# Newton-Schulz sets of a two-layer kernel: turned tiles only streamed, and each turn one transfer to memory and one back

## The chip, the cores and the metric

The kernel runs on one core of a Trainium2 chip. The metric is the device time of one execution in microseconds (us); of the kernel before there are three runs, and one more execution that was profiled.

## The reference

Two layers act on `x` of shape (32, 32, 128, 128) in float32: 32 batches of 32 channels, each channel a 128x128 matrix. The first layer is the one that the change touches. Per matrix it computes an approximate matrix square root by five Newton-Schulz steps:

```python
A2 = gn(x).reshape(b * c, 128, 128)        # group norm over pairs of channels
normA = sqrt(sum(A2 * A2)); Y = A2 / normA; Z = I
for _ in range(5):
    T = 0.5 * (3.0 * I - Z @ Y)
    Y = Y @ T
    Z = T @ Z
x = x + Y * sqrt(normA)
```

The second layer is a spectral convolution: a group norm, a 2-D Fourier transform of which 32 x 64 frequencies are kept, a product over channels with two weight tensors, the inverse transform and a sum with `x`.

## The kernel before, in words

**Sets.** The first layer goes by sets of four channels: a tile is [128 rows, 4, 128]. There are 32 x 8 = 256 sets. The five steps are folded into a few products per set (`newton`, line 447): a quartic polynomial `q` of the matrix, `y = q m`, the next matrix `m = q y`, a second quartic, a last product pair and `t`. A product needs one factor with its rows as the contracted dimension, so at some points a matrix is needed in transposed form. `products` (line 345) runs four 128x128 matmuls into one of eight accumulator banks (`bank`, line 179); its first argument is stationary in TensorE, its second is streamed. In the profile's names `ps<-my,q` the streamed tile stands first and the stationary one second. Each float32 matmul stands in the profile as two instructions, so one call of `products` is 8 of them.

**Near and far.** Batches 1 to 18 are *far* (`is_far`, line 357): 144 sets. The other 112 are *near* and transpose on TensorE. A far set has the transposition done by VectorE and the DMA queues. VectorE transposes within 32x32 blocks straight from the accumulator bank into a tile `turn` (`across`, line 420), and four DMAs of 64 KB on SyncE's queue then move each group of 32 partitions of `turn` to its place in `w` or `mb`. There are three such trips in a far set: one in each of its two quartics (`far_quartic`, line 431, into `w`) and one for the next matrix (line 464, into `mb`). `w` keeps its blocks side by side and is read by TensorE as a strided stream; `mb` is laid out straight, since it is used as a stationary factor, so its transfers write runs of 32 floats.

**Subtractions.** GpSimd computes `eye - matrix` (`minus`, line 340): once in `staged` (line 402), twice in place on the second factor, once on the next matrix (line 466). VectorE adds a product to it (line 436) and forms `q`, `t` and the sum with `x` (`plus`, line 329).

**Order.** Every instruction stays in the order in which the program issues it, per engine. The main loop (line 1090) makes rounds over 8 lanes; a lane holds one set and takes one step of its generator per round, to the next `yield`. `rest` is two yields. A far set has 23 yields and a new one starts every `FAR` = 23/8 rounds. So the yields between two instructions of a set say how many rounds of other work lie between them. From a transposition to the product that streams or holds its result there are four in every trip. `settle` (line 496) stores the finished set to `mid` on SyncE's queue, and loads of `x` go on ScalarE's queue (`fetch`, line 366). Buffers of a tile's name rotate by the numbers in `rooms` (line 308), the second number being extra ones for the first part of the kernel.

**The end of a set.** One 256-wide streamed matmul (line 478) multiplies `q` with `y` and `m` together into two banks, ScalarE takes `m`'s half in two pieces (`t`) and `y`'s in four, and two more products end the set.

Of the kernel before, what the change touches and what calls it, by code (L numbers as in the profile page):

```python
# [29 lines left out]
F32 = mybir.dt.float32  # L30
AF = mybir.ActivationFunctionType
ALU = mybir.AluOpType
# [4 lines left out]
P = 128  # L37
# [11 lines left out]
MS = 1 / QR  # L49
# [44 lines left out]
def conv_preact_kernel(  # L94
# [19 lines left out]
    nc.vector.tensor_scalar_mul(eye1[:, 0, :], ident, EYE)  # L114
    eye = eye1.to_broadcast([P, 4, P])
    eyes = []
    for n, f in (("v", EYE_V), ("q", EYE_Q), ("p", EYE_Q * TURNED)):
        e = const.tile([P, 1, P], F32, name=f"eye_{n}")
        nc.vector.tensor_scalar_mul(e[:, 0, :], ident, f)
        eyes.append(e.to_broadcast([P, 4, P]))  # L120
# [98 lines left out]
    def kept(issued):  # L219
        return issued  # L220

    def prep(bs, made):

        n = len(bs)
        nc_, ng = n * C, n * G
        first_b = bs[0]
        st = small.tile([P, ng, 6], F32, tag="a_st", name=f"a_st{first_b}", bufs=2)
        tiles = []
        parts = [(b, i) for b in bs for i in range(C // 4)]

        ahead = 3 if first_b else 8

        def load(k):
            b, i = parts[k]
            if first_b or i < 4:
                t = stp.tile([P, 2, 2 * P], F32, tag="xs", name=f"xs{b}_{i}")
            else:
                t = four("turn", True).rearrange("p (j c) x -> p j (c x)", j=2)
            src = xs_in[b, :, 2 * i : 2 * i + 2].rearrange("p g h c -> p g (h c)")
            kept(nc.scalar.dma_start(out=t, in_=src))  # L240
            tiles.append(t)

        for k in range(ahead):
            load(k)
        yield
        for k in range(len(parts)):
            for j in range(2):
                nc.vector.bn_stats(st[:, 2 * k + j, :], tiles[k][:, j, :])
            yield
            if k + ahead < len(parts):  # L250
                load(k + ahead)
        ms = small.tile([P, ng], F32, tag="a_ms", name=f"a_ms{first_b}")
        nm, d = yield from moments(st, ms, "a")
        yield from pause
        pq = bank()[:, 0, 0:nc_]
        nc.tensor.matmul(pq, avg_mean, d.rearrange("p g c -> p (g c)"), start=True, stop=True)
        if not first_b:
            warm(5)

        v = small.tile([P, nc_ + ng], F32, tag="a_v", name=f"a_v{first_b}")  # L260
        nc.vector.tensor_scalar_mul(v[:, 0:nc_], pq, -512 / (P * P))
        yield
        vg = small.tile([P, ng], F32, tag="a_vg", name=f"a_vg{first_b}")
        nc.vector.tensor_reduce(
            vg, v[:, 0:nc_].rearrange("p (g c) -> p g c", c=2), AX.X, ALU.add
        )
        nc.vector.tensor_scalar(v[:, nc_:], vg, 0.5, EPS, ALU.mult, ALU.add)
        yield
        s = small.tile([P, nc_ + ng], F32, tag="a_r_s", name=f"a_r_s{first_b}", bufs=2)
        yield from root(v, nc_ + ng, s)  # L270
        iv = small.tile([P, nc_ + ng], F32, tag="a_inv", name=f"a_inv{first_b}")
        nc.vector.reciprocal(iv, s)
        yield

        sc = small.tile([P, nc_], F32, tag="a_sc", name=f"a_sc{first_b}", bufs=2)
        nc.vector.tensor_scalar_mul(sc, iv[:, 0:nc_], MS / P)
        off = small.tile([P, ng, 2], F32, tag="a_off", name=f"a_off{first_b}", bufs=2)
        nc.vector.tensor_tensor(
            off,
            sc.rearrange("p (g c) -> p g c", c=2),  # L280
            nm[:, :, None].to_broadcast([P, ng, 2]),
            ALU.mult,
        )
        off = off.rearrange("p g c -> p (g c)")
        sn = small.tile([P, nc_], F32, tag="a_t_s", name=f"a_t_s{first_b}", bufs=3)
        for k, b in enumerate(bs):
            g, c = slice(k * G, k * G + G), slice(k * C, k * C + C)
            made[b] = (nm[:, g], sc[:, c], off[:, c], sn[:, c])
        yield
        nn = small.tile([P, ng, 2], F32, tag="a_d", name=f"a_n{first_b}")  # L290
        nc.vector.tensor_tensor(
            nn,
            s[:, 0:nc_].rearrange("p (g c) -> p g c", c=2),
            iv[:, nc_:, None].to_broadcast([P, ng, 2]),
            ALU.mult,
        )
        nn = nn.rearrange("p g c -> p (g c)")
        for far in sorted({is_far(b) for b in bs}):
            of = [k for k, b in enumerate(bs) if is_far(b) == far]
            c = slice(of[0] * C, of[-1] * C + C)  # L300
            f = EYE_Q * QS * TURNED**2 if far else EYE * QF
            nc.vector.tensor_scalar_mul(nn[:, c], nn[:, c], P * (1.5 / f) ** 2)
        yield
        yield from root(nn, nc_, sn)
        yield


    rooms = dict(b=(4, 4), xt=(10, 4), x=(3, 2), r=(4, 0), v=(3, 4), w=(3, 2), q=(4, 2))
    rooms.update(my=(4, 2), mb=(2, 3), t=(3, 2), y4=(2, 2), turn=(0, 4))
    turns = dict.fromkeys(rooms, 0)  # L310

    def four(tag, more):
# [27 lines left out]
    def minus(eye, m, t):  # L340

        nc.gpsimd.tensor_tensor(t, eye, m, ALU.subtract)
        return t
# [13 lines left out]
    def is_far(b):  # L357
        return 0 < b < FIRST
# [15 lines left out]
    def staged(b, g, nm, sc, off, sn):  # L374
# [10 lines left out]
        for j in range(4):  # L385
# [13 lines left out]
                on_scalar(m[:, j, :], xt[:, j, :], off, sc, c)  # L399
            on_scalar(mb[:, j, :], mb[:, j, :], off, sc, c)  # L400
            yield
        v = minus(eye_v, m, four("v", True)) if is_far(b) else None
        ready.append((xt, m, mb, v))
        yield

# [11 lines left out]
        yield from rest  # L417
        return q

    def across(ps, more, into):  # L420


        t = four("turn", more)
        nc.vector.transpose(blocks(t), ps.rearrange("p c (i b) -> p b c i", b=4))
        for a in range(4):
            src = t[32 * a : 32 * a + 32].rearrange("p c x -> p (c x)")
            kept(
                nc.sync.dma_start(out=into(a), in_=src.rearrange("p (b x) -> p b x", b=4))
            )

    def far_quartic(m, mb, v, more, f, eye_q):

        ps = products(mb, m)
        w = four("w", more)
        across(ps, more, lambda a: w.rearrange("p c x -> p (c x)")[:, P * a : P * a + P])
        nc.vector.scalar_tensor_tensor(v, ps, 1 / (9 * MS * f), v, ALU.mult, ALU.add)
        minus(eye_q, mb, mb)
        yield from rest
        yield from rest
        ps = products(v, blocks(w).rearrange("p a c j -> p c a j"))  # L440
        q = plus(ps, 9 / (39 * MS**2), mb, "q", more)
        yield from rest
        return q

# [2 lines left out]
    def newton(g, sn, xt, m, mb, v, far, more):  # L447


        qf = QS if far else QF  # L450
        if far:
            q = yield from far_quartic(m, mb, v, more, 1.0, eye_q)
        else:
            q = yield from near_quartic(m, mb, more)
        my = four("my", more)
        y = my[:, :, 0, :]
        nc.scalar.mul(y, products(q, m), 1 / (MS * qf))
        yield from rest
        m = my[:, :, 1, :]
        ps = products(q, y)  # L460
        nc.scalar.mul(m, ps, MS / qf)
        if far:
            mb = four("mb", more)
            across(ps, more, lambda a: mb[:, :, 32 * a : 32 * a + 32])
            yield from rest
            v = minus(eye_v, m, four("v", more))
            yield from rest
            qf, et, eye_t = QS * TURNED, EYE_Q * TURNED, eye_p
            q = yield from far_quartic(m, mb, v, more, TURNED, eye_p)
        else:  # L470
            yield from rest
            mb = taken(transposed(m), "mb", more)
            yield from rest
            et, eye_t = EYE, eye
            q = yield from near_quartic(m, mb, more)
        both = [bank().rearrange("p (j k) x -> p j k x", k=2) for _ in range(2)]
        for j in range(4):
            nc.tensor.matmul(both[j // 2][:, j % 2], q[:, j], my[:, j], start=True, stop=True)
        w, y = four("t", more), four("y4", more)
        for h in range(2):  # L480
            nc.scalar.mul(w[:, 2 * h : 2 * h + 2, :], both[h][:, :, 1, :], 1 / (MS * qf))
        for j in range(4):
            c = 4 * g + j
            nc.scalar.mul(y[:, j, :], both[j // 2][:, j % 2, 0, :], sn[:, c : c + 1])
        yield from rest
        t = plus(products(w, q), -0.5 * et / (1.5 * qf), eye_t, "t", more)
        yield from rest
        nc.vector.tensor_tensor(xt, products(t, y), xt, ALU.add)
        if not todo and lanes.count(None) == LANES - 1:
            warm(2)  # L490
        yield
# [707 lines left out]
```

## Time and profile before

| | |
|---|---|
| three runs | median 3038.55 us, 3033.91 to 3040.33 |
| the profiled execution's own time | 3030.63 us |
| its span, first to last instruction | 3028.5 us |
| TensorE clock granted, mean | 0.984 |
| busy, PE / weight loads / VectorE / ScalarE / GpSimd | 2856.4 / 2636.7 / 2271.7 / 1567.5 / 1995.5 us |
| DMA packets | 746612, 598.69 MB, mean 198 GB/s |
| far sets, first staged to last transfer | about 80 to 1570 us |

The names on the page are those of the program. All compute instructions carry one line (L88, the helper that keeps the order), so rows are told apart by their tiles. PE is the matmul stream, PEld the weight loads that overlap it. SPq stands for instructions that SyncE's sequencer issues, DMAs above all. The time in a row after the second bar is idle time of that engine just before these instructions, and the arrow names what ended it.

### The profile page before, as it was taken

The page shows a single profiled execution, that of the slowest core. Times are in us where ns is not written, and L with a number is a line of the kernel's source. Part 1 is how long each engine was busy: PE and PEld are TensorE (multiplying, and loading weights), DVE is VectorE, ACT ScalarE, POOL GpSimd, SP SyncE. Part 2 cuts the span into 40 slices and gives each one's busy share as a digit, 9 for nine tenths or more (in the row PEclk, how much of TensorE's full clock was granted, in tenths as well). Part 3 has the DMA queues.
Part 4 walks back from the last instruction along what each step waited for, and adds up shares of the span by engine and source line. Part 5 has one row for each costly group of instructions (what it writes and reads, how often), then busy time and mean ns, then how long its engine had stood idle before and what let it go on. Part 6 is the DMA issues. An engine that isn't in the chain of part 4 may idle for free.

```text
span 3028.5 us, 73234 instructions
## 1 busy us (share of the span) xinstructions
PE 2856.4 (94%) x26536; PEld 2636.7 (87%) x26536; DVE 2271.7 (75%) x4407; ACT 1567.5 (52%) x4043; POOL 1995.5 (66%) x2308
## 2 busy tenths in 40 slices
PE   7999999999999999999999999999989999999996
PEld 7999988989989898898899889888878899888884
DVE  7878787878878787878776645877886867777564
ACT  4555555555545555555544445555554544555452
POOL 4677766777767676777665534787777754678352
PEclk9999999999999999999999999999999999999997
DMA  5577777778676877777753566877867747666676
GB/s 178 153 202 173 197 181 178 185 181 205 165 199 166 210 167 204 171 204 174 199 137 99 160 208 206 269 245 252 274 231 253 246 123 214 214 220 216 179 223 247
DMA packets 746612, 598.69 MB, mean 198 GB/s; under 512 B 403472, under 2 KB 564240, under 8 KB 746256
## 3 DMA queue, kind: packets, MB, share of 16 engines
q1 hardware_dynamic: 632640, 385.56, 46.9%
q10 hardware_dynamic: 113616, 208.45, 21.7%
q8 instruction: 215, 3.52, 0.5%
q14 instruction: 141, 1.16, 0.1%
HBM read 326.93 MB, written 153.62 MB: 159 GB/s over the span
## 4 chain that ended last, share of the span: by engine, by line
PE 51%; DMA 17%; DVE 10%; POOL 9%; issue 5%; SPq 5%; ACT 2%; ACTq 1%; DVEq 0%; POOLq 0%
PE ps L88 51%; SPq L88 5%; DMA w<-turn 4%; DMA mb<-turn 3%; POOL yt L88 3%; DMA yt<-mid 2%; DMA mid<-xt 2%; POOL r L88 2%; POOL fold L88 2%; DVE turn L88 2%; POOL x L88 2%; DMA xs<-in_xs 1%; DVE v L88 1%; DVE yt L88 1%; DVE q L88 1%
## 5 line engine op out<-in xcount | busy, mean ns | idle before, releaser
L88 PE MATMUL ps<-my,q 128*128 128x128 f32 (+1 forms) x4096 | 749.7, 331 | 41.3 <-ACT my L88 21.0
L88 PEld LDWEIGHTS ps<-my,q 128*128 128x128 f32 x4096 | 623.6, 192 | 94.7 <-ACT my L88 23.6
L88 ACT ACTIVATE b<-b,a_off,a_sc 128x128 f32<-128x128 f32 x1024 | 467.9, 491 | 348.3 <-DMA b<-in_x 63.8
L88 PE MATMUL ps<-w,v 128*128 128x128 f32 x4096 | 550.4, 279 | 40.5 <-DVE w L88 15.9
L88 PEld LDWEIGHTS ps<-w,v 128*128 128x128 f32 x4096 | 499.7, 193 | 56.6 <-issue 23.4
L88 POOL TENSOR_TENSOR fold<-xt 128x256 f32<-128x256 f32 x512 | 363.7, 733 | 247.1 <-DVE xt L88 220.6
L88 ACT ACTIVATE my<-ps 128x512 f32<-128x512 f32 x512 | 305.7, 599 | 413.9 <-PE ps L88 386.3
L88 POOL TENSOR_TENSOR yt<-yt,d 128x512 f32<-128x512 f32 x244 | 306.8, 1282 | 221.5 <-ACT d L88 190.5
L88 DVE STREAM_TRANSPOSE turn<-ps 128x512 f32<-128x512 f32 x432 | 302.8, 705 | 178.4 <-ACT my L88 102.1
L88 POOL TENSOR_TENSOR v<-eye_v,x 128x512 f32<-128x512 f32 x144 | 183.6, 1275 | 262.7 <-ACT x L88 255.7
L88 POOL TENSOR_SCALAR x<-xt,a_nm,a_sc 128x128 f32<-128x128 f32 x736 | 324.9, 457 | 15.1 <-DVE a_sc L88 14.8
L88 ACT ACTIVATE t<-ps 128x256 f32<-128x256 f32 x512 | 186.9, 380 | 268.9 <-PE ps L88 255.6
L88 ACT ACTIVATE y<-ps,a_t_s 128x128 f32<-128x128 f32 x1024 | 291.4, 375 | 0.0
L88 PE MATMUL ps<-my,mb 128*128 128x128 f32 x2048 | 275.5, 278 | 10.7 <-DMA mb<-turn 4.8
L88 PE MATMUL ps<-x,b 128*128 128x128 f32 x2048 | 281.3, 280 | 1.1 <-ACT b L88 1.0
L88 PE MATMUL ps<-x,q 128*128 128x128 f32 x2048 | 277.5, 279 | 4.6 <-DVE q L88 2.6
L88 PE MATMUL ps<-q,t 128*128 128x128 f32 x2048 | 275.0, 278 | 6.8 <-ACT t L88 6.2
L88 PEld LDWEIGHTS ps<-my,mb 128*128 128x128 f32 x2048 | 259.8, 193 | 22.1 <-issue 9.1
L88 PE MATMUL ps<-y,t 128*128 128x128 f32 x2048 | 275.0, 278 | 0.3 <-DVE b_r L88 0.3
L88 POOL TENSOR_TENSOR mb<-eye_p,mb 128x512 f32<-128x512 f32 x144 | 184.0, 1278 | 133.1 <-PE ps L88 130.9
L88 PEld LDWEIGHTS ps<-x,q 128*128 128x128 f32 x2048 | 252.2, 194 | 15.9 <-issue 8.4
L88 PEld LDWEIGHTS ps<-q,t 128*128 128x128 f32 x2048 | 251.1, 193 | 9.2 <-ACT t L88 7.3
(132 smaller groups left out, 4776.4 us busy)
## 6 DMA issues: line engine op xcount, KB each, us to landing
w<-turn SPq DMA_DIRECT2D x1152, 64.0 KB
b<-in_x ACTq DMA_DIRECT2D x256, 256.0 KB
xt<-in_xt ACTq DMA_DIRECT2D x256, 256.0 KB
mid<-xt SPq DMA_DIRECT2D x256, 256.0 KB
yt<-mid SPq DMA_DIRECT2D x128, 512.0 KB
xs<-in_xs ACTq DMA_DIRECT2D x252, 256.0 KB
out<-yt SPq DMA_DIRECT2D x115, 512.0 KB
mb<-turn SPq DMA_DIRECT2D x576, 64.0 KB
```

The source lines that it names most:

```text
L88: return self.tc.keep_in_program_order(issue(*args, **kw))
```

## The change

It touches far sets only.

- The roles of the two factors are exchanged in the products of a far set: what was held stationary after a turn is now streamed (`products(mb, m)` becomes `products(m, mb)`), and the subtraction in place is made on the other factor. Tiles that came by a trip (`w`, `mb`) are both kept with their blocks side by side and read through `by_rows`.
- `across` is replaced by three functions: `turned` (the same transposition), `away` (one 256 KB DMA from `turn` to a buffer in memory) and `back` (one 256 KB DMA from there, issued two yields later). Both are on SyncE's queue. 12 buffers in memory rotate.
- In the second quartic the subtraction that makes `v` reads the turned tile by rows, and it is issued with the product in place of two yields ahead of it; the addition on VectorE comes one yield later.
- The 256-wide matmul of far sets becomes two 128-wide products with `q` stationary; ScalarE takes the first in one piece.
- Two more early buffers (`b`, `mb`).

```diff
-    rooms = dict(b=(4, 4), xt=(10, 4), x=(3, 2), r=(4, 0), v=(3, 4), w=(3, 2), q=(4, 2))
-    rooms.update(my=(4, 2), mb=(2, 3), t=(3, 2), y4=(2, 2), turn=(0, 4))
+    rooms = dict(b=(4, 5), xt=(10, 4), x=(3, 2), r=(4, 0), v=(3, 4), w=(3, 2), q=(4, 2))
+    rooms.update(my=(4, 2), mb=(2, 4), t=(3, 2), y4=(2, 2), turn=(0, 4))
...
-        v = minus(eye_v, m, four("v", True)) if is_far(b) else None
+        v = minus(eye_v, mb, four("v", True)) if is_far(b) else None
...
-    def across(ps, more, into):
+    def turned(ps, more):
         t = four("turn", more)
         nc.vector.transpose(blocks(t), ps.rearrange("p c (i b) -> p b c i", b=4))
-        for a in range(4):
-            src = t[32 * a : 32 * a + 32].rearrange("p c x -> p (c x)")
-            kept(
-                nc.sync.dma_start(out=into(a), in_=src.rearrange("p (b x) -> p b x", b=4))
-            )
+        return t
+
+    def away(t):
+        held = dram.tile([P, 512], F32, name="turn", tag="turn", bufs=12)
+        kept(nc.sync.dma_start(out=held, in_=t.rearrange("p c x -> p (c x)")))
+        return held
+
+    def back(held, tag, more):
+        t = four(tag, more)
+        src = held.rearrange("(a i) (b x) -> (i b) a x", a=4, b=4)
+        into = t.rearrange("p c x -> p (c x)").rearrange("p (a x) -> p a x", a=4)
+        kept(nc.sync.dma_start(out=into, in_=src))
+        return t
+
+    def by_rows(t):
+        return blocks(t).rearrange("p a c j -> p c a j")
 
-    def far_quartic(m, mb, v, more, f, eye_q):
-        ps = products(mb, m)
-        w = four("w", more)
-        across(ps, more, lambda a: w.rearrange("p c x -> p (c x)")[:, P * a : P * a + P])
-        nc.vector.scalar_tensor_tensor(v, ps, 1 / (9 * MS * f), v, ALU.mult, ALU.add)
-        minus(eye_q, mb, mb)
-        yield from rest
+    def far_quartic(m, mb, v, f, later, more):
+        ps = products(m, mb)
+        held = away(turned(ps, more))
+        minus(eye_q, m, m)
+        if later:
+            yield
+        nc.vector.scalar_tensor_tensor(v, ps, 1 / (9 * MS), v, ALU.mult, ALU.add)
+        if not later:
+            yield
+        yield
+        w = back(held, "w", more)
         yield from rest
-        ps = products(v, blocks(w).rearrange("p a c j -> p c a j"))
-        q = plus(ps, 9 / (39 * MS**2), mb, "q", more)
+        q = plus(products(v, by_rows(w)), 9 / (39 * MS**2 * f**2), m, "q", more)
         yield from rest
         return q
...
         if far:
-            mb = four("mb", more)
-            across(ps, more, lambda a: mb[:, :, 32 * a : 32 * a + 32])
+            held = away(turned(ps, more))
+            nc.scalar.mul(m, ps, MS / qf)
             yield from rest
-            v = minus(eye_v, m, four("v", more))
+            mb = back(held, "mb", more)
             yield from rest
-            qf, et, eye_t = QS * TURNED, EYE_Q * TURNED, eye_p
-            q = yield from far_quartic(m, mb, v, more, TURNED, eye_p)
+            v = four("v", more)
+            form = "p c (a j) -> p c a j"
+            minus(eye_p.rearrange(form, a=4), by_rows(mb), v.rearrange(form, a=4))
+            q = yield from far_quartic(m, by_rows(mb), v, TURNED, True, more)
+            w, y4 = four("t", more), four("y4", more)
+            nc.scalar.mul(w, products(q, by_rows(mb)), 1 / (MS * qf * TURNED))
+            ps = products(q, y)
+            for j in range(4):
+                c = 4 * g + j
+                nc.scalar.mul(y4[:, j, :], ps[:, j, :], sn[:, c : c + 1])
```

More of the change, by code (lines that the diff above doesn't have):

```diff
@@ L116, in conv_preact_kernel @@
     eyes = []
-    for n, f in (("v", EYE_V), ("q", EYE_Q), ("p", EYE_Q * TURNED)):
+    for n, f in (("v", EYE_V), ("q", EYE_Q), ("p", EYE_V * TURNED)):
         e = const.tile([P, 1, P], F32, name=f"eye_{n}")
@@ L300, in prep @@
             c = slice(of[0] * C, of[-1] * C + C)
-            f = EYE_Q * QS * TURNED**2 if far else EYE * QF
+            f = EYE_Q * QS if far else EYE * QF
             nc.vector.tensor_scalar_mul(nn[:, c], nn[:, c], P * (1.5 / f) ** 2)
@@ L447, in newton @@
     def newton(g, sn, xt, m, mb, v, far, more):
-        qf = QS if far else QF
+        qf, et, eye_t = (QS, EYE_Q, eye_q) if far else (QF, EYE, eye)
         if far:
-            q = yield from far_quartic(m, mb, v, more, 1.0, eye_q)
+            q = yield from far_quartic(m, mb, v, 1.0, False, more)
         else:
@@ L456, in newton @@
         y = my[:, :, 0, :]
-        nc.scalar.mul(y, products(q, m), 1 / (MS * qf))
+        nc.scalar.mul(y, products(q, mb if far else m), 1 / (MS * qf))
         yield from rest
         m = my[:, :, 1, :]
-        ps = products(q, y)
-        nc.scalar.mul(m, ps, MS / qf)
+        ps = products(y, q) if far else products(q, y)
         if far:
-            mb = four("mb", more)
-            across(ps, more, lambda a: mb[:, :, 32 * a : 32 * a + 32])
+            held = away(turned(ps, more))
+            nc.scalar.mul(m, ps, MS / qf)
             yield from rest
-            v = minus(eye_v, m, four("v", more))
+            mb = back(held, "mb", more)
             yield from rest
-            qf, et, eye_t = QS * TURNED, EYE_Q * TURNED, eye_p
-            q = yield from far_quartic(m, mb, v, more, TURNED, eye_p)
+            v = four("v", more)
[8 more added lines that the diff above has]
+                nc.scalar.mul(y4[:, j, :], ps[:, j, :], sn[:, c : c + 1])
         else:
+            nc.scalar.mul(m, ps, MS / qf)
             yield from rest
@@ L473, in newton @@
             yield from rest
-            et, eye_t = EYE, eye
             q = yield from near_quartic(m, mb, more)
[L476 to L484, printed above, removed]
+            both = [bank().rearrange("p (j k) x -> p j k x", k=2) for _ in range(2)]
+            for j in range(4):
+                nc.tensor.matmul(both[j // 2][:, j % 2], q[:, j], my[:, j], start=True, stop=True)
+            w, y4 = four("t", more), four("y4", more)
+            for h in range(2):
+                nc.scalar.mul(w[:, 2 * h : 2 * h + 2, :], both[h][:, :, 1, :], 1 / (MS * qf))
+            for j in range(4):
+                c = 4 * g + j
+                nc.scalar.mul(y4[:, j, :], both[j // 2][:, j % 2, 0, :], sn[:, c : c + 1])
         yield from rest
@@ L487, in newton @@
         yield from rest
-        nc.vector.tensor_tensor(xt, products(t, y), xt, ALU.add)
+        ps = products(y4, t) if far else products(t, y4)
+        nc.vector.tensor_tensor(xt, ps, xt, ALU.add)
         if not todo and lanes.count(None) == LANES - 1:
```

## The prediction

> **What bounds the kernel now.** I read the busy time of the whole span first, then that of a stretch which holds far sets alone (200 to 1500 us), then what TensorE waited for in that stretch, then its rows by shape, and last SyncE's queue.
>
> ```profile
> PE 2856.4 (94%) x26536; PEld 2636.7 (87%) x26536; DVE 2271.7 (75%) x4407; ACT 1567.5 (52%) x4043; POOL 1995.5 (66%) x2308
> ```
>
> ```profile
> 200.00:1500.00 1300.00, 1245.36 (x10202) 1171.38 (x10200) 1065.65 (x2109) 706.66 (x1882) 931.42 (x1027) 0.99 0.75 187
> ```
>
> In the far stretch PE is busy 1245 of 1300 us, VectorE 82%, ScalarE 54%, GpSimd 72%, the 16 DMA engines 75%. The stretch issues 512 of the 576 `mb` transfers, four to a set: 128 sets, 10.16 us each, so a round (one set per 23/8 rounds) is 3.53 us. TensorE sets the pace, and what a change here can give is bounded by the 55 us in which it is idle. Its waits in this stretch:
>
> ```profile
> PE ps L88 <- ACT my L88: 13.6, 7, 3.3
> PE ps L88 <- DMA mb<-turn: 11.8, 9, 3.5
> PE ps L88 <- DVE q L88: 10.0, 11, 1.3
> PE ps L88 <- DMA xt<-in_xt: 5.6, 4, 1.7
> PE ps L88 <- ACT t L88: 3.4, 3, 2.3
> PE ps L88 <- DMA w<-turn: 3.3, 4, 1.8
> ...
> PE ps L88 <- DVE turn L88: 1.8, 1, 1.8
> ```
>
> Columns are us, times, longest. The trips of turned tiles (`mb`, `w`, `turn`) make 16.9 us; with the issue gap at each I count 19. The rows by shape of the same stretch:
>
> ```profile
> L88 PE MATMUL ps<-my,q 128*128 128x256 f32 x1028 | 244.6, 381 | 9.0 <-DVE q L88 8.9
> ...
> L88 PE MATMUL ps<-my,q 128*128 128x128 f32 x1032 | 138.5, 277 | 14.1 <-ACT my L88 13.6 <-DVE v L88 0.4
> L88 PE MATMUL ps<-my,mb 128*128 128x128 f32 x1024 | 137.7, 278 | 10.1 <-DMA mb<-turn 4.8 <-issue 2.0 <-DVE turn L88 1.8
> ```
>
> Mean durations overlap, so I took start-to-start times from the same records: median 112 ns for a 128-wide instruction, 216 ns for a 256-wide one. SyncE's queue in one stretch of the timeline (start, us, what, how many):
>
> ```profile
> 1039.67 3.37 SPq L88 DMA_DIRECT2D mb<-turn  x4
> 1043.14 5.15 SPq L88 DMA_DIRECT2D w<-turn  x8
> 1049.54 3.51 SPq L88 DMA_DIRECT2D mb<-turn  x4
> 1053.10 0.62 SPq L88 DMA_DIRECT2D mid<-xt  x1
> 1054.71 5.10 SPq L88 DMA_DIRECT2D w<-turn  x8
> ```
>
> It issues nearly without a pause: 13 issues of about 0.64 us in a set's 10.16. I matched every transposition with its four issues, their landing (last semaphore step of the DMA) and the product that needs them. Medians for `w`: 2.8 us from the end of the transposition to the first issue, 2.5 for four issues, 1.9 from the last issue to landing, and then 3.2 us of slack until the product (mean 3.1; in 5% of the trips 0.1, which are the waits above). For `mb`: 0.6, 2.8, 2.8 and 3.9 of slack. From transposition to product it is 11.4 us (`w`) and 10.2 (`mb`).
>
> **What the Trainium skill says.** "DMA: Bandwidth & Descriptors", section "Specifications", wants 512 B or more per descriptor for line rate. The trace agrees: in the stretch, packets of 128 B took 13 ns (median), of 512 B 27, of 2 KB 84, which is 10, 19 and 24 GB/s per engine; but a 128 B packet is still the cheapest one to have. The same page, "Latency and other measured facts", gives HBM access as 0.2 us, 2 us at high load. The store `mid<-xt`, 256 KB to memory, landed in 2.3 us at the 5th percentile, 3.4 median, 5.0 at the 95th: a spread of that size. The same page, "Two DMAs through the same engine are not ordered", says that the issuer must wait for the first transfer's semaphore before it issues one that reads what it wrote; so SyncE must wait for each `away`. The trace has no such pair in the turns. "TensorE: Matmul & The Clock Gate", section "Wait — 56ns, not 53.3ns?", puts a fixed 2.5 ns on a matmul; here 2 x 112 - 216 = 8 ns, and I use the 8.
>
> **The change part by part.**
>
> *The split matmul.* Per far set 8 instructions of 216 ns become 16 of 112: +64 ns, on the engine that sets the pace; x 144 = +9 us. Weight loads grow by 8 per set and stay under the stream (PEld 1171 against 1245). Streaming `mb` by rows should be free: `w` was streamed so and has the same 112 ns.
>
> *ScalarE.* Two `t` pieces of 380 ns become one 512-wide of about 599: -0.16 us per set on an engine at 54%: nothing. In staging, `v` now waits for the last `b` piece and not the last `x` piece, 0.5 us; rounds of other work cover it.
>
> *GpSimd.* Four subtractions of 1.28 us before and after. The second `v` is now made with the product rather than two rounds ahead, and VectorE needs it one round (3.5 us) later. GpSimd waited 103.6 us for PE at this place (80 times), so it has room for 1.28 us: nothing, at most 0.5 us for one set in five (14 us). By-rows reading there was not in the trace; equal cost is likely, as inner runs are contiguous.
>
> *VectorE.* Same work: three transpositions (0.71 us), two additions (0.65). The second one a round later holds its bank longer. From a `my,mb` product to the eighth bank request after it is 7.55 us (minimum 6.7). The addition now ends about 0.9 + 3.5 + 0.65 = 5.1 us plus VectorE's lag after the product; that lag is 0.04 us median, 2.0 at the 75th percentile, 3.4 at the 95th. So it is late in about one set in five, by some 0.5 us: 14 us if all count. I take +5, ends 0 and 15. Queued behind a late addition would be the next transposition.
>
> *SyncE's queue.* 12 issues per set become 6: from 13 x 0.64 = 8.3 to 7 x 0.64 = 4.5 us in 10.16. It waits longer instead: `back` waits for its `away` to land, and queued behind it are the next `away`, other sets' `back` and `mid<-xt`.
>
> *DMA engines.* Per set the turns took 1024 packets x 33.8 ns (mean) + 2048 x 13.8 = 63 engine-us (66 by totals per set). Now 3 x (128 x 89.2 + 512 x 33.8) = 86: the share goes from 0.75 to about 0.87 (0.80 if packets took their medians). The byte count of the turns doubles.
>
> *The trip itself*, which decides. Its four rounds are unchanged. In the new order of SyncE's queue, an `mb` return stands behind two later `away`, a `w` return mostly behind one (180 of 240; none in 30, two in 30). SyncE issues in order, so a return cannot go before VectorE has transposed those other sets, however soon its own tile has landed. I laid this order over the instants of the trace before (ends of transpositions, 0.6 us per issue, 3.4 us for a landing in memory as `mid<-xt`, 3.8 for the return as the loads `xt<-in_xt`, median 3.9, and `b<-in_x`, 3.4). The return is then issued 5.7 us (`w`) and 4.8 (`mb`) after the transposition, median, 8.6 and 7.3 at the 95th percentile, and lands 3.8 later. Slack to the product: median 1.6 us for `w`, 2.2 for `mb`, and 95 of 384 trips late, by 60 + 45 = 105 us in all. Before it was 3.2 and 3.9. So the second landing costs more than the six spared issues. The 105 us are not all lost: 3 x 11 / 10.2 = 3.2 trips are in flight at a time, and a stall for one gives the same time to the others. I count a third, 35 us, and take off 10, half of the 19 that trips cost already, since SyncE's backlog behind them goes: +25 in this stretch, x 144/128 = +28. Ends: -21 (all 19 x 1.125 gone) and, if lateness is hardly shared, +110.
>
> *Sum* against the profiled execution: 3030.6 (2.1 above its span, start and end, unchanged) + 9 + 5 + 28 = 3073. The median of the runs stands 8 above that execution: **3081 us**, 1.4% slower.
>
> **The rivals.**
>
> *SyncE's relief wins.* If both legs land near their floor (2.3 and 3.0 us) and VectorE's lag shrinks, returns come in time. Then the 19 us of trip waits go, and half of the waits for `my` and `q` (23.6) that follow from late trips: 31 x 1.125 = 35, less the 9 of the split: 3013, faster. For it: SyncE was busy 8.3 of 10.2 us and 2.8 us behind for `w`, and the same overlay of the old order gives 5 us of slack where the trace had 3.1 to 3.5, so backlog costs more than my overlay tells. Against: the order of the queue holds returns back by a whole transposition of another set. It decides from the point where transposition to landing is under some 8 us (5th percentile of the time until the product: 8.2 for `w`, 7.7 for `mb`).
>
> *The DMA engines become the bound.* At 0.87 share, legs land in 4.0 and 4.5: 125 + 69 = 194 us late, a third is 65, less 10, x 1.125 = 62; the loads come late as well (ScalarE waited 55.5 us for `b<-in_x` already), +20. With 9 and 5: 3135.
>
> *It is hidden anyway.* Trips late as often as now: 9 us of split, less some: 3042, no change.
>
> **How the numbers follow.** Late returns 0.47 (3050 to 3112), DMA-bound 0.15, relief 0.27, hidden 0.11. A measurement of this kernel can tell about 0.2%, 6 us, from no change. Faster 0.27, same 0.11, slower 0.62. Range 3012 to 3150: below lies half of the relief case, above the worst of the DMA-bound one.
>
> **What would show it.** Right: PE waits for `mb<-turn` and `w<-turn` in the far stretch grow from 15 us to 35 or more; SyncE's longest waits are for transpositions, with a return queued behind; the stretch of far sets grows by 35 to 45 us and the rest not at all; DMA share there 0.80 to 0.87; no 256-wide `my,q` rows of far sets; PE waits for `v` appear, a few us. Wrong: slack after landing of 3 us or more; PE waits for DMAs under 10 us; or GpSimd's by-rows subtraction over 1.5 us, which would make VectorE's addition the wait.

## The result and the profile after

| | before | after |
|---|---|---|
| median of the runs | 3036.41 us (4) | 3177.74 us (4; 3157.59 to 3178.41) |
| ratio, 95% interval | | 1.0448, 1.0405 to 1.0491 |
| profiled execution, span | 3028.5 us | 3176.6 us |
| last `mb` transfer of a far set starts | 1558 us | 1698 us |
| a far set, in 200 to 1500 us | 10.16 us (128 sets) | 11.11 us (117 sets) |
| PE idle per far set there | 0.43 us | 1.14 us |
| PE busy per far set there | 9.73 us | 9.97 us |

The change makes the kernel 4.5% slower. The direction was forecast, the size was not: 3177.74 lies above the range. Of the 148 us between the two spans 140 are there by the last `mb` transfer, so the loss is in the far sets. The lines of the profile after that answer to those shown of before, first the busy times of the span, then of the far stretch:

```profile
PE 2900.2 (91%) x27688; PEld 2705.4 (85%) x27688; DVE 2266.5 (71%) x4407; ACT 1558.3 (49%) x3899; POOL 1997.8 (63%) x2308
```

```profile
200.00:1500.00 1300.00, 1166.95 (x10200) 1121.44 (x10201) 961.62 (x1922) 636.62 (x1597) 853.63 (x937) 0.97 0.78 243
```

Every engine is less busy in the far stretch than before, PE too, and no engine has become the bound. The DMA engines are at 0.78 (0.75 before). The column before that is TensorE's granted clock, 0.97 where it was 0.99. What PE waited for (us, times, longest):

```profile
PE ps L88 <- DMA w<-turn: 92.6, 57, 5.0
PE ps L88 <- DMA mb<-turn: 37.3, 25, 3.0
PE ps L88 <- DVE a_st L88: 3.4, 2, 2.8
PE ps L88 <- DVE q L88: 0.5, 1, 0.5
```

The trips cost PE 130 us where they cost 17, which is 1.11 us a far set in place of 0.13. All other idle time of PE has all but gone (0.03 us a set in place of 0.30), since nothing else is last any more. The rows by shape of the same stretch show on which product it falls, and that the streamed `mb` costs what other streams cost:

```profile
L88 PE MATMUL ps<-w,v 128*128 128x128 f32 x1886 | 261.6, 285 | 93.4 <-DMA w<-turn 92.6 <-DVE a_st L88 0.6
...
L88 PE MATMUL ps<-mb,my 128*128 128x128 f32 x936 | 128.3, 281 | 40.5 <-DMA mb<-turn 37.3 <-DVE a_st L88 2.8 <-DVE q L88 0.5
...
L88 PE MATMUL ps<-mb,q 128*128 128x128 f32 x936 | 124.3, 276 | 0.0
L88 PE MATMUL ps<-my,q 128*128 128x128 f32 x936 | 123.6, 275 | 0.0
```

SyncE's queue in this stretch is no longer busy issuing: its issues take 391 us, where they took 1086. It waits, above all for transpositions:

```profile
SPq L88 <- DVE turn L88: 605.2, 302, 8.6
SPq L88 <- DMA turn<-turn: 93.1, 74, 4.6
```

The second row is the wait of a return for its own first leg, the first is the wait of an `away` for its transposition, with returns of other sets behind it. The chain of waits from 1000 to 1030 us (start, us, what) runs through SyncE's queue twice:

```profile
1002.61 5.25 DMA mb<-turn
1007.85 0.14 issue
1007.99 6.50 PE ps L88 x56
...
1019.72 0.63 DVE turn L88
1020.35 0.02 issue
1020.37 0.33 SPq L88
...
1020.81 5.12 DMA w<-turn
1025.93 0.14 issue
1026.07 4.05 PE ps L88 x23
```

At 1019.72 VectorE transposes for one set; SyncE sends that tile away (0.33 us), and only then issues the return of another set's `w`. It lands 5.12 us later, and ends 3.5 us in which PE stood still for it. I matched every trip in the stretch as I had for the kernel before. For `w`: return issued 6.4 us after its own transposition (median), leg back 4.5, and 72 of 234 trips land with under 0.3 us to spare. For `mb`: 5.2, 4.5, and 29 of 117. In those 72 the first leg had landed over 0.7 us before the return went out in all but 5, and in the median the return went out 0.46 us after the end of the transposition of *another* set. So it is the place in the queue that held these 72, and not the memory that had to be written first.

### The profile page after: what moved, and what is told of

Read it like the earlier page. It is cut to its first block, busy times and chain, and to the rows that moved or that the text cites. A ratio compares the mean times of both kernels' runs of the same rounds, so it can differ in the third digit from the quotient of the medians.

```text
span 3176.6 us, 73722 instructions
## 1 busy us (share of the span) xinstructions
PE 2900.2 (91%) x27688; PEld 2705.4 (85%) x27688; DVE 2266.5 (71%) x4407; ACT 1558.3 (49%) x3899; POOL 1997.8 (63%) x2308
## 4 chain that ended last, share of the span: by engine, by line
PE 58%; DMA 21%; POOL 7%; DVE 6%; issue 4%; ACT 1%; SPq 1%; ACTq 0%; DVEq 0%; POOLq 0%
PE ps L88 58%; DMA w<-turn 9%; DMA mb<-turn 5%; POOL yt L88 2%; POOL x L88 2%; DMA xt<-in_xt 2%; POOL r L88 2%; POOL fold L88 1%; DVE yt L88 1%; DMA xs<-in_xs 1%; SPq L88 1%; DMA out<-yt 1%; DMA yt<-mid 1%; DVE turn L88 1%; DMA plain<-xs 1%
## 5 line engine op out<-in xcount | busy, mean ns | idle before, releaser
L88 PE MATMUL ps<-my,q 128*128 128x128 f32 (+1 forms) x2944 | 474.8, 309 | 14.3 <-DVE q L88 10.2
L88 PEld LDWEIGHTS ps<-my,q 128*128 128x128 f32 x2944 | 414.4, 192 | 41.0 <-issue 11.7
L88 POOL TENSOR_TENSOR v<-eye_v,b 128x512 f32<-128x512 f32 x144 | 183.5, 1274 | 169.9 <-ACT b L88 169.9
L88 ACT ACTIVATE t<-ps 128x256 f32<-128x256 f32 (+1 forms) x368 | 171.0, 466 | 208.0 <-PE ps L88 195.6
L88 POOL TENSOR_TENSOR v<-eye_p,mb 128x512 f32<-128x512 f32 x144 | 183.5, 1274 | 138.1 <-DMA mb<-turn 137.7
L88 POOL TENSOR_TENSOR x<-eye_q,x 128x512 f32<-128x512 f32 x144 | 183.9, 1277 | 120.4 <-PE ps L88 120.4
L88 DVE SCALAR_TENSOR_TENSOR q<-ps,eye 128x512 f32<-128x512 f32 x224 | 153.6, 686 | 135.2 <-PE ps L88 131.2
L88 DVE SCALAR_TENSOR_TENSOR w<-ps,r 128x512 f32<-128x512 f32 x224 | 153.6, 686 | 134.7 <-PE ps L88 73.1
L88 POOL TENSOR_TENSOR my<-eye_q,my 128x512 f32<-128x512 f32 x144 | 183.6, 1275 | 77.3 <-PE ps L88 74.5
L88 DVE BATCH_NORM_STATS2 a_st<-xs 128x6 f32<-128x256 f32 x504 | 185.6, 411 | 50.4 <-DMA xs<-in_xs 50.2
```

Source lines behind the costliest of these rows:

```text
L88: return self.tc.keep_in_program_order(issue(*args, **kw))
```

## The experiments

Each stood beside runs of the kernel before on the same chip (medians 3036.43 for e1 to e4, 3043.66 for e5 to e8, 3040.15 for e9 to e11, 3034.62 for e12), so ratios are compared. "Stretch" is 200 to 1500 us. In the diffs, `...` stands for lines left out, some calls are shortened, and the comments after `#` belong to this text. Three theories were kept apart: *order* (returns stand behind other sets' transfers on SyncE), *legs or load* (two legs through memory are long and burden the DMA engines), *exchange* (the loss is in the exchanged factors, the later subtraction or the split).

**e1_direct: the exchange without the trip through memory.**

```diff
-    def away(t): ...
-    def back(held, tag, more): ...
+    def across(t, tag, more):
+        into = four(tag, more)
+        flat = into.rearrange("p c x -> p (c x)")
+        for a in range(4):
+            src = t[32 * a : 32 * a + 32].rearrange("p c x -> p (c x)")
+            kept(nc.sync.dma_start(out=flat[:, P * a : P * a + P], in_=src.rearrange("p (b x) -> p b x", b=4)))
+        return into
...
-        held = away(turned(ps, more))
+        w = across(turned(ps, more), "w", more)
```

> The exchange of the factors kept; each trip made in four direct transfers of 64 KB into the by-rows layout, issued with the transposition, nothing through memory. Order theory (returns stand behind other sets' transfers) and leg theory (two legs through memory are too long and load the DMA engines) both give about 3045 us (3036 and 9 for the split matmul), PE waits for turned tiles under 25 us in 200 to 1500 us. Exchange theory (the loss is in the exchange of the factors, the later subtraction or the split): above 3100.

3030.08 us, ratio 0.9978 (0.9968 to 0.9989): 0.2% faster than the kernel before, 15 us less than both theories gave, and 148 us faster than the changed kernel. The stretch, and PE's waits in it:

```profile
200.00:1500.00 1300.00, 1253.63 (x11204) 1205.14 (x11204) 1054.58 (x2100) 680.89 (x1745) 929.52 (x1029) 0.99 0.68 187
```

```profile
PE ps L88 <- ACT b L88: 17.6, 21, 2.7
PE ps L88 <- DMA w<-turn: 11.0, 9, 2.1
PE ps L88 <- ACT t L88: 9.4, 13, 2.1
```

Trips make 11.4 us (`mb` 0.4). The exchange theory falls: all that is lost lies in how the tile travels.

**e2_early_return: the return one round sooner.**

```diff
-        yield
-        w = back(held, "w", more)
+        w = back(held, "w", more)
+        yield
```

and the same for `mb`.

> The changed kernel with each return issued one round after its transposition in place of two, the trip's four rounds kept. Order theory: returns go out some 4.5 us after the transposition in place of 6.3 and 5.2, late trips fall to less than half, 3070 to 3110 us. Leg theory: SyncE then waits for the landing in memory (3.8 us) with the next set's transfers queued behind it, so those go later by what the return gains: 3150 to 3200.

3147.45 us, ratio 1.0361 (1.0345 to 1.0376). That lies outside both ranges: 30 us less than the changed kernel, far from the order theory's 3110 and just under the leg theory's 3150.

```profile
PE ps L88 <- DMA mb<-turn: 74.4, 35, 4.7
PE ps L88 <- DMA w<-turn: 20.9, 27, 2.1
```

```profile
SPq L88 <- DMA turn<-turn: 598.0, 268, 6.3
```

The returns hardly go out sooner: 5.7 us after the transposition for `w` in place of 6.4, and 5.2 for `mb` as before. 74 of 356 trips are late, where 101 of 351 were. Returns go out 0.06 us (median) after their first leg has landed. SyncE now waits for the landing (598 us, 93 in the changed kernel), and the next set's `away`, which used to leave 0.03 us after its transposition, leaves 1.1 us after it on average. Lateness moves from `w` to `mb`. The place in the queue and the landing of the first leg are two ends of one trade, as the leg theory said here; both follow from one queue in order.

**e3_five_rounds: a fifth round for each trip.**

```diff
         w = back(held, "w", more)
+        yield
         yield from rest
...
-        yield from rest          # after q, and after y of far sets
+        yield
```

> The changed kernel with five rounds for each trip, the fifth taken from the two rounds after q or y; 23 steps as before. If lateness of the returns is the whole loss, by either theory: PE waits for turned tiles under 30 us in 200 to 1500 us and 3045 to 3070 us, unless waits for q or y take their place (then PE waits for DVE q or ACT my of 30 us or more). If DMA load or the exchange costs by itself: above 3120.

3077.98 us, ratio 1.0136 (1.0121 to 1.0152).

```profile
PE ps L88 <- ACT my L88: 33.6, 30, 1.8
PE ps L88 <- DVE q L88: 29.9, 32, 1.7
PE ps L88 <- DMA mb<-turn: 19.1, 11, 3.0
PE ps L88 <- DMA w<-turn: 5.0, 6, 1.4
```

Trip waits fall from 130 to 24 us, and 64 us of waits for `q` and `my` take their place, on the steps that were shortened. That is the exception which the expectation named. Lateness was the greater part of the loss; the round had to come from somewhere.

**e4_return_on_act: the return on another queue.**

```diff
-        kept(nc.sync.dma_start(out=into, in_=src))
+        kept(nc.scalar.dma_start(out=into, in_=src))
```

> The changed kernel with the returns issued on ScalarE's queue. Order theory: a return no longer stands behind other sets' transfers on SyncE, and goes out when ScalarE reaches it: 3060 to 3110 us. Leg theory: the legs and the DMA load are the same, 3150 to 3190. ScalarE is in order too: where a return waits there for its first leg or for ScalarE's own backlog, my and t come late, which would show as PE waits for ACT and a time above 3180.

3065.10 us, ratio 1.0092 (1.0077 to 1.0107): inside the order theory's range. One word takes back 113 of 141 us, with every byte still going through memory. The far stretch, PE's waits and SyncE's longest:

```profile
200.00:1500.00 1300.00, 1232.95 (x10959) 1188.08 (x10961) 1023.53 (x2054) 673.88 (x1714) 914.14 (x1007) 0.98 0.83 258
```

```profile
PE ps L88 <- DMA mb<-turn: 49.2, 31, 3.1
PE ps L88 <- DMA w<-turn: 11.4, 21, 1.1
```

```profile
SPq L88 <- DVE turn L88: 784.8, 342, 6.2
```

The DMA engines are at 0.83, higher than in the changed kernel (0.78), since sets pass faster. The two legs together take 8.3 us for `w` and 7.4 for `mb` (sums of medians), where they took 8.7 and 7.7. So neither the load of the DMA engines nor the length of the legs by itself made the changed kernel as slow as it is. SyncE still waits 785 us for transpositions, now with no return behind them. PE waits 61 us for trips, less than half of the 130: four rounds are still tight for two landings.

**e7_halves_late: the order without the memory.**

```diff
+        held, w = turned(ps, more), four("w", more)
+        across(held, w, (0, 1))
...
         yield
+        across(held, w, (2, 3))      # at the place of the return
```

> e1_direct, but of a trip's four direct transfers two go at once and two are issued two rounds later, at the place of the return: so nothing goes through memory and the bytes are those of e1_direct, but half of each trip stands behind other sets' transfers that wait for their transpositions. Two more turn tiles. Order theory: the late half is issued some 5 us after the transposition and lands about 3.5 us later, 1.5 us sooner than a return: 3060 to 3120 us and PE waits for turned tiles of 50 us or more in 200 to 1500 us. Leg theory: 3030 to 3040.

3169.63 us, ratio 1.0415 (1.0393 to 1.0437). Nothing goes through memory, the DMA share is 0.63, the bytes are those of e1_direct, and nearly the whole loss of the changed kernel is back.

```profile
200.00:1500.00 1300.00, 1169.94 (x10251) 1124.65 (x10252) 963.91 (x1930) 638.25 (x1601) 853.86 (x938) 0.98 0.63 172
```

```profile
PE ps L88 <- DMA mb<-turn: 50.0, 23, 4.9
PE ps L88 <- DMA w<-turn: 42.0, 38, 3.1
```

It is slower than I expected (3060 to 3120): the late half goes out 7.7 us (`w`) and 6.7 us (`mb`) after its transposition and not some 5, since SyncE also has its 13 issues of 0.6 us per set here, so a late half stands behind issues as well as waits. 95 of 352 trips are late, much as in the changed kernel. Of PE's 130 us of idle time 92 are for trips; the rest, for ScalarE, VectorE and loads, the changed kernel did not have. With e4 this settles what made the trips late: late places on the queue are enough without memory, and trips through memory with the returns on another queue cost 0.9%.

**e11_act_early: both remedies.** The return on ScalarE's queue and one round sooner.

```diff
-        kept(nc.sync.dma_start(out=into, in_=src))
+        kept(nc.scalar.dma_start(out=into, in_=src))
...
-        yield
-        w = back(held, "w", more)
+        w = back(held, "w", more)
+        yield
```

> e4_return_on_act and e2_early_return together: returns on ScalarE's queue and one round sooner. If queue order and the place of the return are all that makes trips late: a trip then takes two landings, 8.5 us, against 11 to 12 until the product, PE waits for turned tiles fall under 30 us in 200 to 1500 and the time to 3035 to 3050 us. If two landings are too long by themselves: 3060 or more. ScalarE may wait for the first landing, up to 1 us each time.

3096.06 us, ratio 1.0173 (1.0145 to 1.0201). Trip waits are 27 us, as said; the time is not. (The profiled execution is the fastest of the four, 3077.11 us.) A return now goes out, in the median, within 0.1 us of the landing of its first leg, so ScalarE waits for first legs, and what it does for others comes late:

```profile
PE ps L88 <- DMA mb<-turn: 15.0, 13, 2.6
PE ps L88 <- ACT my L88: 12.3, 13, 2.3
PE ps L88 <- DMA w<-turn: 12.3, 13, 2.3
PE ps L88 <- ACT t L88: 11.8, 15, 1.6
```

GpSimd waits 272 us for ScalarE's `b`, where it waited 168 in e4. A queue that also computes is a poor place to wait.

**e5_direct_loaded, e9_loads_beside, e12_one_big_load: the load alone.** Three attempts to load the DMA engines beside the trips of e1_direct as the memory trips do. They add transfers that nobody reads; outputs stay as they are.

```diff
+        # e5, for each trip, SyncE: a store of the turned tile, and later a load
+        kept(nc.sync.dma_start(out=held, in_=t.rearrange("p c x -> p (c x)")))
+        kept(nc.sync.dma_start(out=spare_tile, in_=x[b, :, 0:32:8, :]))
+        # e9, for each far set, ScalarE: twice
+        kept(nc.scalar.dma_start(out=u, in_=x[B - 1, :, k:32:8, :]))
+        # e12, for each far set, SyncE: once
+        kept(nc.sync.dma_start(out=u, in_=x[B - 1, :, 0:8, :]))
```

> The direct trips of e1_direct, and beside each the traffic of a trip through memory for which nobody waits: one 256 KB store of the turned tile and one 256 KB load in runs of 512 B into a spare tile, on SyncE's queue at the places of away and back. DMA share then rises to about 0.9 or more and SyncE issues 19 times a set. Order theory: landings come later by the load alone, 3035 to 3070 us. Load theory (it is the added traffic that makes transfers late): 3100 or more.

> e1_direct with two further loads of 256 KB per far set in runs of 512 B, on ScalarE's queue beside the set's own loads, into spare tiles that nothing reads: some 1.8 us of all 16 engines per set, which is what the trips through memory add to the direct ones, with SyncE's queue and the order left alone (e5_direct_loaded loaded SyncE's queue as well). Order theory: 3030 to 3050 us, DMA share about 0.85. Load theory: above 3100.

> e1_direct with one further load of 512 KB per far set (runs of 4 KB) on SyncE's queue beside mid, into a spare tile that nothing reads: one more issue of some 0.5 us per set, and about 1.6 us of all 16 engines per set, so a DMA share of some 0.84, as the trips through memory have it. This loads the DMA engines without many issues, which e5_direct_loaded and e9_loads_beside did not manage. Order theory: 3030 to 3060 us. Load theory: 3100 or more, with PE waits for turned tiles of 50 us and more in 200 to 1500 us.

e5: 3690.78 us, ratio 1.2132 (1.2101 to 1.2162). e9: 3224.55, 1.0613 (1.0590 to 1.0635). e12: 3201.98, 1.0546 (1.0517 to 1.0576). All three are far slower than the order theory gave, and none measures the load by itself, because each held up the queue that carried it. In e5 a trip's first issue comes 11.8 us after its transposition (median; 2.1 in e1_direct): SyncE had 19 issues in a set. In e9 trips are on time (0.6 us of PE waits in the stretch) and ScalarE is not:

```profile
PE ps L88 <- ACT my L88: 67.8, 25, 6.8
PE ps L88 <- ACT t L88: 51.4, 30, 3.8
PE ps L88 <- ACT b L88: 18.7, 48, 2.5
```

In e9 the load may have a part in it too: ScalarE waits 61 us there for the added loads and 163 for the set's own `xt`. In e12 SyncE waits 126.3 us for the added load to land, with turned tiles queued behind it (first issue 4.0 us after the transposition), and 51 us of trip waits and 56 for ScalarE follow. The DMA share was 0.80, 0.75 and 0.75, no higher than in e4 at 3065 us. So what the load costs by itself stays open; e4 bounds it, together with the longer legs and the late `mb` trips left there, by 35 us (3065.10 less 3030.08).

**e6_split_alone: the split in the kernel before.**

```diff
+        if far:
+            w, y = four("t", more), four("y4", more)
+            nc.scalar.mul(w, products(q, my[:, :, 1, :]), 1 / (MS * qf))
+            ps = products(q, my[:, :, 0, :])
```

> The kernel before with only the 256-wide matmul of far sets split in two 128-wide products, q stationary in both. 144 sets x 64 ns = 9 us by the start-to-start times: 3043 to 3048 us if the split is paid in full; 3036 or less if stalls of other kinds swallow it.

3056.91 us, ratio 1.0050 (1.0034 to 1.0066): 13 us between the medians and 15 by the ratio, with 10 to 20 as its interval, where I had 9.

```profile
200.00:1500.00 1300.00, 1237.10 (x11070) 1190.17 (x11070) 1052.04 (x2072) 689.12 (x1730) 921.15 (x1017) 0.99 0.74 184
```

PE is busy 1237.1 us for 126 sets in the stretch, 9.82 per set against 9.73: 0.09 x 144 = 13 us. The term is right in kind and some 50% short.

**e8_direct_five and e10_direct_wide: two attempts at more than e1_direct.** Five rounds for the direct trips; and `mb` moved straight into the second half of `my`, so that the 256-wide matmul comes back.

```diff
+        yield                        # e8, in each trip; one less after q and y
         yield from rest
...
+            mb = straight(turned(ps, more), my[:, :, 1, :])     # e10
+            m = four("mb", more)
```

> e1_direct with five rounds for each trip, the fifth taken from the two after q or y, to see whether the 11 us of trip waits left in e1_direct can be had. By e3 the shorter step brings PE waits for DVE q and ACT my of some 60 us per 1300: 3050 to 3080 us. If those waits in e3 came from the late trips and not from the shorter step: 3020.

> e1_direct, but the turned next matrix is moved in runs of 32 floats into the second half of my, in place of the matrix itself, which gets a tile of its own; so q is multiplied with both by one 256-wide matmul as in the kernel before. Saves the split, 9 us by start-to-start times and 13 to 15 by e6_split_alone: 3015 to 3025 us, unless the shorter runs bring late mb trips back (the kernel before had 11.8 us of them per 1300): then 3030.

e8: 3116.36 us, ratio 1.0248 (1.0227 to 1.0270), above the 3050 to 3080 expected, with no trip waits and 100 us of waits for `my` and `q` in the stretch: shortening those steps costs far more than the 11 us of trip waits that it removes. e10: 3061.07 us, 1.0072 (1.0053 to 1.0092), where I expected 3015 to 3030: slower than e1_direct though the split is gone. PE waits 19.0 us for `t`, 18.4 for trips and 13.3 for `my` there. Why its `t` and `w` come later than in e1_direct I have not settled. e1_direct stays the fastest kernel of all, 0.22% under the kernel before.

## Why the prediction was right or wrong

**Right: the bound and what made trips late.** PE set the pace, the late returns decided, and they were late for the reason given: the place in SyncE's order. Predicted issue of a return after its transposition was 5.7 (`w`) and 4.8 us (`mb`), measured 6.4 and 5.2. Late trips were to be 95 of 384; 101 of 351 came. Of the signs that were named, PE's waits for trips, SyncE's waits for transpositions and the missing 256-wide rows came. The DMA share stayed below its range, no PE wait for `v` appeared, and the far sets took 140 us more and not 35 to 45.

**Wrong: "I count a third".** The overlay gave 105 us of lateness in the stretch. I divided it by three, because a stall for one trip gives the same time to the others in flight. Measured, lateness was lost nearly whole. Laid over the same instants with the medians that the trace after shows (legs as below, 0.35 us for an issue), the overlay gives about 155 us for its 128 sets, an estimate of 1.2 us a set; PE waited 130 us in 117 sets, 1.1 us a set. A third would have been 0.4.

The likely reason is a circle, argued from the trace and not tested by itself. A return waits on SyncE for the transposition of another set, that waits for a product on PE, and PE is what stands still. When PE stalls, the returns that have not been issued yet move back with it. The chain shown above has its links: transposition, `away`, return, landing, product. For the 72 late `w` trips, product and transposition of the other set take 0.9 and 0.7 us, and 6.6 us (mean) pass from the end of that transposition to the product that needs the return. With VectorE's lags that is 8.2 us or more, while the two products lie about two rounds apart, and two rounds of 3.53 us are 7.06. So the rounds stretched, to 11.11 / 2.875 = 3.86 us on average. e7 shows late trips from the order without memory, and in e4, with the returns on another queue, less than half of the waits is left.

Counted in full, 105 x 1.125 = 118 us would have stood in the sum in place of 39. The prediction named this case as an end of the term (+110, "if lateness is hardly shared"), which makes its sum 3163, but its range stopped at 3150.

**Short: the landings.** I took 3.4 and 3.8 us. Measured medians of the first leg are 4.2 (`w`) and 3.2 (`mb`), of the return 4.5 for both, and 5.5 in the late `w` trips. With 0.35 us for an issue the overlay gives about 80 us at my landings, and the 155 at the measured ones. I had 4.0 and 4.5 for the rival in which the DMA engines bind; it gave 194 us of lateness and was divided by three as well.

**Missing: TensorE's clock.** The sum had no term for it. The Trainium skill, "TensorE: Matmul & The Clock Gate", section "What's actually happening", says that the clock falls to half after an idle window of about 3.4 us. The trace agrees on the length: in the stretch the granted clock was at half in 17 pieces of 3.41 us or twice that, 68 us together, where before it was in 4, 14 us. It differs on how idle a window has to be: in the 3.41 us ahead of these 17 pieces PE was busy for up to 45%, and only 7 of its gaps in the stretch were longer than 3.41 us. So waits that add up to about 2 us within a window were enough. Half of the difference of 68 and 14 is lost where PE works, at most 27 us per 1300. By set, PE is busy 0.24 us longer than before; e1_direct, with the same products and the clock at 0.99, is busy 0.06 longer (9.79). So 0.18 us of each set, 26 us in all, are put down to the clock.

**The sum as it came out.** Per far set +0.71 us of idle PE (trips +0.98, all other waits -0.27, of which the prediction's sum counted none), +0.06 for the split, +0.18 for the clock: 0.95 x 144 = 137 us, of 141.

**The other terms.** The split: 9 us forecast, 13 to 15 measured alone in e6, but e1_direct has it and is faster, since other waits shrink. ScalarE's single `t` (592 ns) cost nothing. GpSimd's by-rows subtraction took 1274 ns, as the plain one. The bank held a round longer (+5): no PE wait for `v` in the stretch of e1_direct, which has the same later addition, so nothing. The DMA engines: 86 engine-us per set for the turns forecast; with the rest of a set that made 142, and 0.78 of 16 engines over 11.11 us is 139, against 122 before. The share itself was to be 0.80 to 0.87; it is lower because a set takes longer. SyncE's issues came shorter than the 0.6 us that I took: 0.33 us for an `away`, 0.38 for a return.

**The rivals.** Relief of SyncE was real (391 us of issues in place of 1086) and gained nothing, since the queue waited for transpositions instead. The DMA-bound case did not come: the share is 0.78, and e4 runs faster at 0.83. What the longer landings owe to the load stays open.

## What to carry to other kernels

On an in-order queue a transfer is as late as what stands before it. Before two-step trips are put on one queue, ask which event the instruction ahead of the second step waits for, and whether that event depends in turn on the engine that waits for the trip: if so, don't count on lateness being shared among the trips in flight; here it was lost nearly whole. A queue that only waits and issues looks idle in the busy times; read its waits and what is behind them. Here, four small direct transfers a trip beat one large pair through memory by 148 us.

## What the runs showed of the hardware that was not expected

- SyncE needs 0.33 to 0.39 us to issue a 256 KB transfer between a tile and memory, and 0.60 to 0.63 us for a 64 KB one from 32 partitions to 128 between tiles: the larger transfer is the quicker one to issue.
- Short waits of PE cost twice. 130 us of waits of up to 5.0 us in 1300 brought 68 us at half clock; before, 55 us of idle time with waits of up to 3.5 us had left it at 14.
- No whole window has to be idle for that. In the stretch of all 14 traces, cut into windows of 3.41 us in step with the pieces at half clock, each of the 157 windows at full clock in which PE was busy under 40% was followed by half clock, and 1 of the 4793 in which it was busy over half; between the two, 46 of 97 were. In e1_direct no wait was longer than 2.7 us, and the clock was at half for 18 us.
- Filling the DMA engines to 0.75 or 0.80 by transfers that nobody reads cost 5 to 21%, with the queue that issued them held up; a higher share with the returns on another queue (e4, 0.83) cost 0.9%.
